# The order of a layer norm and MLP stage written out by hand, with part of its elementwise work moved to GpSimd

## The chip, the cores and the metric

The kernel runs on one core of a Trainium2 chip. The metric is the device time of one execution in microseconds (us); the time of a version is the median of several runs. The core has a matrix engine (TensorE, PE in the profile, with its weight loads as PEld), VectorE (DVE), ScalarE (ACT), GpSimd (POOL) and a queue engine that starts transfers (SyncE, SP). Each engine works through its own queue of instructions in order, and they wait for each other by semaphores. Matmul results land in PSUM, in banks of 512 f32 values for each of 128 partitions; everything else is in SBUF.

## The reference, cut to what matters

Four samples of 56 x 56 pixels with 128 channels go through four layers: a block of attention and MLP over windows, an edge layer, a spectral attention layer and a convolution, each behind a normalization. The change concerns only the second half of the first layer, which comes after its attention. For every pixel, with `h` the 128 values after attention and `x` the block's input:

```
n   = (h - mean(h)) / sqrt(var(h) + 1e-5) * g2 + be2       # over the 128 channels of a pixel
mlp = gelu(n @ w1 + b1) @ w2 + b2                          # 128 -> 512 -> 128
y   = h + mlp + x                                          # two residuals
```

The next layer normalizes `y` by groups of channels over the whole sample, so it needs the mean and variance of `y`.

## The kernel before, in words

All data is f32. `first_layers` runs once for each of the four samples, one after the other: `fast_attention`, then `mlp` (L848), then `edge_layer` (L905). Channels lie on the 128 partitions; a sample is a row of 3136 pixels in window order. `xf` holds `h`, `xw` holds `x`, and `x1` receives `y` in image order, from where the edge layer reads it. (A second branch of the program, for inputs with large scores, calls the same `mlp` and isn't executed.)

`mlp` cuts the sample into eight parts of 392 pixels, each a row of eight 7 x 7 windows. It has two stages:

- *The norm stage* (loop at L870). A matmul with a centring matrix subtracts the mean (`centre`, L676, matmul L679, into one of four PSUM banks `mm`). ScalarE squares the result into `n_sq` (L681) and copies it into `y` (L874). A second matmul averages the squares over the partitions (L689, into one of two banks `v`), ScalarE takes the square root (L691), VectorE the reciprocal (L692), and VectorE multiplies `y` by it (L877). The gains `g2` and `be2` are folded into the weights.
- *The MLP stage* (loop at L879). `hidden` (L860) makes four matmuls of a part (L864, into the banks `mm`) and four Gelu activations on ScalarE (L865). It is called for the part after the current one before the four matmuls of the current part with `w2` (L885), which add up in one of two banks `acc`, named `m_po`. VectorE then makes `h + b2 + x` in SBUF (L886) and adds it to the PSUM result while it puts the windows in image order: a large add for seven of the eight windows (343 pixels, L892) and two small ones for the eighth, which wraps around the side of the image (28 and 21 pixels, L894 and L895). A statistics instruction on the finished rows follows (L896). The last part goes in two pieces of four and three rows, since it wraps around the image.

A matmul of this size is two passes in the profile, so four matmuls are shown as "x8". TensorE's order is the program's order (`manual_schedule`, L868); the orders of ScalarE and VectorE in `mlp` are made by a list scheduler when the program is built. GpSimd has no work in `mlp`. ScalarE loads a table of functions when it turns from one to another: for the square root at L691, for Gelu at L865, and again for the square root by a dummy activation at L898. After `mlp`, `group_norm_factors` (L2348 to L2360) reduces the statistics, and the edge layer begins (L939).

Of the kernel before, what the change touches and what calls it, by code (L numbers as in the profile page):

```python
# [11 lines left out]
F32 = mybir.dt.float32  # L12
AF = mybir.ActivationFunctionType
ALU = mybir.AluOpType
# [4 lines left out]
P = 128  # L19
B = 4  # L20
HH = 56
# [651 lines left out]
        output(NBLK - 1, pm[:, :NB])  # L673


def centre(k, pool, centred, src, squares, j):  # L676

    nc = k.nc
    nc.tensor.matmul(centred, k.centre, src, start=True, stop=True)  # L679
    squares[j] = pool.tile([P, centred.shape[1]], F32, tag="sq", name="n_sq")  # L680
    nc.scalar.activation(squares[j], centred, AF.Square)  # L681


def inverse_deviation(k, pool, psum, squares, bufs=2):

    nc = k.nc
    n = squares.shape[1]
    pv = psum.tile([P, 512], F32, tag="v", name="n_pv")
    nc.tensor.matmul(pv[:, :n], k.ones_c, squares, start=True, stop=True)  # L689
    r = pool.tile([P, n], F32, tag="rs", name="n_r", bufs=bufs)  # L690
    nc.scalar.activation(r, pv[:, :n], AF.Sqrt, bias=k.eps)  # L691
    nc.vector.reciprocal(r, r)  # L692
    return r


def attention_bias(k, w, pool):


    nc = k.nc
    with k.tc.tile_pool(name="b_ps", bufs=1, space=PSUM) as psum:  # L700
        ps = psum.tile([P, 512], F32, name="b_p")
        nc.tensor.matmul(ps[:, 0:1], w.wo, w.bv, start=True, stop=True)
        for i, t in enumerate((w.wq, w.wk, w.wv)):
            nc.tensor.matmul(ps[:, 1 + i:2 + i], t, w.be1, start=True, stop=True)
        for f in range(4):
            nc.tensor.matmul(ps[:, 4 + f:5 + f], w.w1[:, f * P:(f + 1) * P], w.be2, start=True, stop=True)
        for n, t, g in (("fq", w.wq, w.g1), ("fk", w.wk, w.g1), ("fv", w.wv, w.g1), ("f1", w.w1, w.g2)):
            f = pool.tile(list(t.shape), F32, name="w_" + n)
            nc.vector.tensor_scalar_mul(f, t, g)
            setattr(w, n, f)  # L710
        for i, (n, bias) in enumerate((("bvo", w.bo), ("fbq", w.bq), ("fbk", w.bk), ("fbv", w.bv))):
            f = pool.tile([P, 1], F32, name="w_" + n)
            nc.vector.tensor_add(f, ps[:, i:i + 1], bias)
            setattr(w, n, f)
        w.fb1 = pool.tile([P, 4], F32, name="w_fb1")
        nc.vector.tensor_add(w.fb1, ps[:, 4:8], w.b1)
        nc.tensor.matmul(ps[:, 8:9], w.wo, w.fbv, start=True, stop=True)
        w.fbvo = pool.tile([P, 1], F32, name="w_fbvo")
        nc.vector.tensor_add(w.fbvo, ps[:, 8:9], w.bo)
# [128 lines left out]
def mlp(k, w, xf, xw, x1, st):  # L848


    nc, tc = k.nc, k.tc
    N = 8 * WIN
    with ExitStack() as es:
        big = es.enter_context(tc.tile_pool(name="m_big", bufs=1))
        wk = es.enter_context(tc.tile_pool(name="m_wk", bufs=2))
        psum = es.enter_context(tc.tile_pool(name="m_ps", bufs=2, space=PSUM))
        y = big.tile([P, TOK], F32, name="m_y")
        parts = [slice(wi * N, (wi + 1) * N) for wi in range(8)]

        def hidden(ts):  # L860
            hT = wk.tile([P, 4, N], F32, name="m_hT")
            for f in range(4):
                ph = psum.tile([P, 512], F32, tag="mm", name="m_ph", bufs=4)
                nc.tensor.matmul(ph[:, :N], w.f1[:, f * P:(f + 1) * P], y[:, ts], start=True, stop=True)  # L864
                nc.scalar.activation(hT[:, f, :], ph[:, :N], AF.Gelu, bias=w.fb1[:, f:f + 1])  # L865
            return hT

        es.enter_context(tc.manual_schedule(engines={mybir.EngineType.PE}))  # L868
        squares = {}
        for wi in range(9):  # L870
            if wi < 8:
                pc = psum.tile([P, 512], F32, tag="mm", name="m_pc", bufs=4)
                centre(k, wk, pc[:, :N], xf[:, parts[wi]], squares, wi)
                nc.scalar.copy(y[:, parts[wi]], pc[:, :N])  # L874
            if wi:
                yb = y[:, parts[wi - 1]]
                nc.vector.tensor_mul(yb, yb, inverse_deviation(k, wk, psum, squares.pop(wi - 1), 8))  # L877
        ahead = hidden(parts[0])
        for wi, ts in enumerate(parts):  # L879
            hT = ahead  # L880
            if wi < 7:
                ahead = hidden(parts[wi + 1])
            po = psum.tile([P, 512], F32, tag="acc", name="m_po")
            for f in range(4):
                nc.tensor.matmul(po[:, :N], w.w2[:, f, :], hT[:, f, :], start=(f == 0), stop=(f == 3))  # L885
            nc.vector.scalar_tensor_tensor(xf[:, ts], xf[:, ts], w.b2, xw[:, ts], ALU.add, ALU.add)  # L886
            a = xf[:, ts].rearrange("p (w i j) -> p w i j", w=8, i=7)
            x = po[:, :N].rearrange("p (w i j) -> p w i j", w=8, i=7)
            for i0, i1 in (((0, 7),) if wi < 7 else ((0, 4), (4, 7))):
                r0 = (7 * wi + 3 + i0) % HH  # L890
                rows = x1[:, r0:r0 + i1 - i0, :]
                nc.vector.tensor_add(  # L892
                    rows[:, :, 3:52].rearrange("p i (w j) -> p w i j", w=7), a[:, 0:7, i0:i1, :], x[:, 0:7, i0:i1, :])
                nc.vector.tensor_add(rows[:, :, 52:56], a[:, 7, i0:i1, 0:4], x[:, 7, i0:i1, 0:4])  # L894
                nc.vector.tensor_add(rows[:, :, 0:3], a[:, 7, i0:i1, 4:7], x[:, 7, i0:i1, 4:7])  # L895
                nc.vector.bn_stats(st[:, wi + (i0 > 0), :], rows.rearrange("p l n -> p (l n)"))  # L896

        nc.scalar.activation(wk.tile([P, 1], F32, name="m_root"), hT[:, 3, 0:1], AF.Sqrt, bias=k.eps, scale=0.0)  # L898

# [822 lines left out]
class Plan:  # L1724
# [8 lines left out]
    def add(self, engine, cost, run, after=(), takes=(), gives=(), lag=0.0, table=None):  # L1733
        op = Env()
        op.engine, op.cost, op.run, op.after, op.lag, op.table = engine, cost, run, list(after), lag, table
        op.takes, op.gives, op.end = list(takes), list(gives), None
        self.ops.append(op)
        return op
# [629 lines left out]
def build(k, packs, I, out):  # L2368
# [3 lines left out]
    with ExitStack() as es:  # L2372
# [12 lines left out]
        with tc.tile_pool(name="w01", bufs=1) as wp, tc.tile_pool(name="io", bufs=1) as io:  # L2385
# [30 lines left out]
            def first_layers(attention, x, to, loaded=False):  # L2416
                if not loaded:
                    nc.sync.dma_start(xw, x)
                xf = io.tile([P, TOK], F32, name="xf")
                attention(k, w0, xw, xf)  # L2420
                st = io.tile([P, 9, 6], F32, name="x1_st")
                mlp(k, w0, xf, xw, x1, st)
                edge_layer(k, w1, x1, st)
                nc.sync.dma_start(to, x1)
# [62 lines left out]
```

## Time and profile before

| what | value |
|---|---|
| median of 7 runs | 3905.01 us (3888.44 to 3908.33) |
| the profiled execution: own time, span of its instructions | 3898.99 us, 3897.2 us |
| busy: PE, DVE, ACT, POOL | 91%, 74%, 54%, 30% of the span |
| mean granted TensorE clock | 0.957 of full |

The span runs from the first instruction to the last; the execution's own time has 1.79 us more around it. Times of instructions are in us from the span's start. Where `mlp` lies in the four samples (us, from the timeline):

| sample | first centring matmul (L679) | first matmul of `hidden` of the second part (L864) | end of the last `w2` matmul (L885) | statistics reduced (L2348) |
|---|---|---|---|---|
| 1 | 535.81 | 551.79 | 595.52 | 597.20 |
| 2 | 1238.24 | 1254.58 | 1298.30 | 1299.98 |
| 3 | 1941.56 | 1957.81 | 2001.53 | 2003.22 |
| 4 | 2649.02 | 2664.98 | 2706.85 | 2708.54 |

So `mlp` takes some 61 us of each sample, about 245 us of the 3897. In a line of the timeline the first number is the start, the second the length, then come engine, line of the kernel, operation, destination and sources with their sizes and the number of instructions merged; in brackets stands the idle time before it and what ended that.

### The profile page before, as it was taken

Reading aid. Unit: us, or ns where it says so; the run is one execution under the profiler, and the core shown is the slowest. Engines: PE = TensorE matmul, PEld = TensorE weight load, DVE = VectorE, ACT = ScalarE, POOL = GpSimd, SP = SyncE. Lnnn points to the kernel's source line nnn. Section 1 sums busy time; section 2 is a strip of 40 time slices with the busy share of each in tenths; the row PEclk is TensorE's granted clock in tenths of the full one; section 3 lists DMA queues with packets and bytes.
Section 4 is the critical chain, followed back from the end, with each engine's and each line's share of the span. In section 5 each row is a group of like instructions: output and inputs, shape, how many; then the busy total and the mean of one; then the engine's idle time right before and its main releaser. Section 6 shows DMA issues by size and latency. Waiting matters only on the chain. (4 is left out here: it accounts for less than half of the span.)

```text
span 3897.2 us, 79417 instructions
## 1 busy us (share of the span) xinstructions
PE 3542.5 (91%) x35416; PEld 1593.6 (41%) x35416; DVE 2890.3 (74%) x2759; ACT 2086.6 (54%) x2108; POOL 1157.0 (30%) x563
## 2 busy tenths in 40 slices
PE   6899989989998898999889999998967989999988
PEld 4322234543223445222245532224446433336554
DVE  6588877758897784888778578886965767775664
ACT  4577755557786445877655467774622012215332
POOL 0000006500000470000037100001851768984665
PEclk8999999999999999999999999999978999999988
DMA  2000000000000000000000000000031048841101
GB/s 95 1 1 1 1 17 2 19 1 1 1 1 1 18 19 1 1 1 1 1 18 3 18 1 1 1 1 1 3 107 67 1 100 170 171 109 65 59 9 50
DMA packets 73497, 111.13 MB, mean 29 GB/s; under 512 B 62140, under 2 KB 63932, under 8 KB 67900
## 3 DMA queue, kind: packets, MB, share of 16 engines
q1 hardware_dynamic: 14460, 93.13, 8.1%
q10 hardware_dynamic: 58688, 12.85, 2.0%
q8 instruction: 280, 4.59, 0.5%
q14 instruction: 69, 0.57, 0.0%
HBM read 79.46 MB, written 26.51 MB: 27 GB/s over the span
## 5 line engine op out<-in xcount | busy, mean ns | idle before, releaser
L651 ACT ACTIVATE f_ring<-f_s 128x1792 f32<-128x1792 f32 (+3 forms) x796 | 1097.8, 1430 | 230.4 <-PE f_s L649 228.5
L594 DVE TENSOR_TENSOR f_acc<-f_acc,f_ring 128x1792 f32<-128x1792 f32 x560 | 1134.0, 2025 | 65.9 <-ACT f_ring L651 9.1
L988 POOL TENSOR_TENSOR e_tp<-e_a,e_c 128x1792 f32<-128x1792 f32 x140 | 451.6, 3258 | 2285.7 <-ACT e_a L951 2179.7
L649 PE MATMUL f_s<-f_qT,f_kT 32*128 32x448 f32 x5376 | 739.9, 572 | 48.1 <-ACT f_ring L651 28.3
L600 PE MATMUL f_po<-f_ring,f_va 128*32 128x448 f32 x5376 | 592.0, 548 | 0.0
L986 DVE TENSOR_TENSOR e_td<-e_pa,e_c 128x1792 f32<-128x1792 f32 x252 | 491.3, 2013 | 14.2 <-ACT e_a L951 14.2
L649 PEld LDWEIGHTS f_s<-f_qT,f_kT 32*128 32x128 f32 x5376 | 268.5, 183 | 526.7 <-ACT f_ring L651 383.1
L993 PE MATMUL e_acc<-e_td,t_shared 32*32 32x448 f32 x8064 | 323.0, 546 | 22.7 <-DVE e_td L986 11.7
L990 ACT ACTIVATE e_tp<-e_tp 128x1792 f32<-128x1792 f32 x140 | 235.1, 1697 | 176.5 <-POOL e_tp L988 176.5
L1589 DVE TENSOR_TENSOR u_ud<-u_px,u_d 112x1792 f32<-112x1792 f32 x144 | 240.1, 1707 | 95.3 <-PE u_po L1594 86.3
L600 PEld LDWEIGHTS f_po<-f_ring,f_va 128*32 128x32 f32 x5376 | 133.0, 109 | 398.5 <-issue 397.6
L993 PE MATMUL e_acc<-e_tp,t_shared 32*32 32x448 f32 x4480 | 221.9, 547 | 3.1 <-ACT e_tp L990 2.5
L1594 PE MATMUL u_po<-u_ud,AT 112*64 112x448 f32 x960 | 200.7, 548 | 23.3 <-DVE u_ud L1589 23.3
L1591 POOL TENSOR_TENSOR u_up<-xh,u_d 112x1792 f32<-112x1792 f32 x64 | 193.8, 3052 | 24.5 <-PE u_po L1594 12.9
L993 PEld LDWEIGHTS e_acc<-e_td,t_shared 32*32 32x32 f32 x8064 | 133.6, 103 | 147.1 <-DVE e_td L986 57.0
L617 DVE RECIPROCAL f_den<-f_den 128x448 f32<-128x448 f32 x28 | 82.7, 2953 | 77.5 <-ACT f_den L616 77.5
L1594 PE MATMUL u_po<-u_up,AT 112*64 112x448 f32 x576 | 125.0, 541 | 1.0 <-POOL u_up L1591 1.0
L1594 PEld LDWEIGHTS u_po<-u_ud,AT 112*64 112x64 f32 x960 | 64.8, 137 | 147.6 <-issue 86.6
L594 DVE TENSOR_TENSOR f_acc<-f_ring 128x1792 f32<-128x1792 f32 x28 | 56.7, 2024 | 89.2 <-ACT f_ring L651 60.3
L865 ACT ACTIVATE m_hT<-m_ph,w_fb 128x392 f32<-128x392 f32 x128 | 72.7, 589 | 84.3 <-PE m_ph L864 78.9
L993 PEld LDWEIGHTS e_acc<-e_tp,t_shared 32*32 32x32 f32 x4480 | 94.9, 103 | 55.5 <-ACT e_tp L990 19.5
L1678 ACT COPY x_ev<-x_po 56x896 f32<-56x896 f32 x32 | 28.8, 901 | 155.6 <-DMA xm<-x_ev 83.9
(467 smaller groups left out, 4763.3 us busy)
## 6 DMA issues: line engine op xcount, KB each, us to landing
u_d<-dd SPq DMA_DIRECT2D x48, 784.0 KB
xw<-in_x SPq DMA_DIRECT2D x4, 1568.0 KB
x2d<-x SPq DMA_DIRECT2D x4, 1568.0 KB
x_xs<-xad ACTq DMA_DIRECT2D x32, 196.0 KB
xm<-x_ev ACTq DMA_DIRECT2D x64, 98.0 KB
o_a<-xm SPq DMA_DIRECT2D x8, 784.0 KB
o_x<-x2d SPq DMA_DIRECT2D x4, 1568.0 KB
out<-o_o SPq DMA_DIRECT2D x12, 448.0 KB
```

What stands on the lines that cost most here:

```text
L594: nc.vector.tensor_add(acc, slots(j, 0) if c == 1 else acc, slots(j, c))
L600: nc.tensor.matmul(po[heads[h], :NB], va[o, c, heads[h]], p, start=(c == 0), stop=(c == 24))
L617: nc.vector.reciprocal(den[:, 0], den[:, 0])
L649: nc.tensor.matmul(ss[:, i, :NB], kT[heads[h], c * P:(c + 1) * P], qT[heads[h], blk(j)], start=True, stop=True)
L651: nc.scalar.activation(ring[:, slot:slot + m, :], ss[:, :m, :NB], AF.Exp, scale=scale)
L986: nc.vector.tensor_tensor(t, am, cm, ALU.max)
L988: nc.gpsimd.tensor_sub(t, bc(a.rearrange("p (l n) -> p l n", l=8), 1, 4), cm)
L990: nc.scalar.activation(tf, tf, AF.Relu)
L993: nc.tensor.matmul(acc[quarters[q], r, :NB], k.ident[o, o], t[o, q].rearrange("p l n -> p (l n)"), start=(g == 0), stop=(g == len(EDGE_TUR ...
L1589: nc.vector.tensor_mul(u, bc(px[:, :, :NB], 2, m), dm)
L1591: nc.gpsimd.tensor_mul(u, bc(x, 2, m), dm)
L1594: nc.tensor.matmul(po[64 * b2:64 * b2 + 64, :NB], st.AT[:, 8 * i + h0 + q, 2 * bp + b2, :], u[:, b2, q, :], start=(left == 16), stop=(left ...
```

## The change

Only `mlp` is changed; `centre` and `inverse_deviation`, which nothing else calls, are written into it.

- ScalarE and VectorE now follow the program's order in `mlp` too, like TensorE.
- The table of the square root is loaded by a dummy activation at the beginning of `mlp`. In ScalarE's queue of the built program it stands ahead of the last copy of the attention (`f_den`, L616); it waits for the last matmul of L608.
- Of the first four parts ScalarE squares the centred values, and VectorE copies them into `y`. Of the last four ScalarE copies them, and GpSimd squares the copy. The second matmul of a part follows its centring matmul at a distance of one for the first four parts and of two for the others.
- The reciprocals and multiplications of the parts 0 to 2 stand behind the four copies on VectorE; that of part `wi + 3` stands behind the `w2` matmuls of part `wi`.
- For the parts 0 to 6 VectorE adds PSUM, `b2` and `h` into SBUF in one instruction, and GpSimd adds `x` and puts the result in image order with three adds. Statistics of a part follow one turn later. Only the last part is written as before, its six adds ahead of its two statistics instructions.
- The load of the next sample's `xw` (L2418) now waits for GpSimd's last adds and for the last part's `h + b2 + x`.

```diff
@@ -673,26 +673,6 @@
         output(NBLK - 1, pm[:, :NB])
 
 
-def centre(k, pool, centred, src, squares, j):
-
-    nc = k.nc
-    nc.tensor.matmul(centred, k.centre, src, start=True, stop=True)
-    squares[j] = pool.tile([P, centred.shape[1]], F32, tag="sq", name="n_sq")
-    nc.scalar.activation(squares[j], centred, AF.Square)
-
-
-def inverse_deviation(k, pool, psum, squares, bufs=2):
-
-    nc = k.nc
-    n = squares.shape[1]
-    pv = psum.tile([P, 512], F32, tag="v", name="n_pv")
-    nc.tensor.matmul(pv[:, :n], k.ones_c, squares, start=True, stop=True)
-    r = pool.tile([P, n], F32, tag="rs", name="n_r", bufs=bufs)
-    nc.scalar.activation(r, pv[:, :n], AF.Sqrt, bias=k.eps)
-    nc.vector.reciprocal(r, r)
-    return r
-
-
 def attention_bias(k, w, pool):
 
 
@@ -865,37 +845,88 @@
                 nc.scalar.activation(hT[:, f, :], ph[:, :N], AF.Gelu, bias=w.fb1[:, f:f + 1])
             return hT
 
-        es.enter_context(tc.manual_schedule(engines={mybir.EngineType.PE}))
-        squares = {}
-        for wi in range(9):
+        es.enter_context(tc.manual_schedule(engines={mybir.EngineType.PE, mybir.EngineType.Activation,
+                                                     mybir.EngineType.DVE}))
+        squares, roots = {}, {}
+        root = wk.tile([P, 1], F32, name="m_root")
+        nc.scalar.activation(root, k.eps, AF.Sqrt)
+
+        def central(wi):
+
+            pc = psum.tile([P, 512], F32, tag="mm", name="m_pc", bufs=4)
+            yb = y[:, parts[wi]]
+            nc.tensor.matmul(pc[:, :N], k.centre, xf[:, parts[wi]], start=True, stop=True)
+            squares[wi] = wk.tile([P, N], F32, name="m_sq", bufs=3)
+            if wi < 4:
+                nc.scalar.activation(squares[wi], pc[:, :N], AF.Square)
+                nc.vector.tensor_copy(yb, pc[:, :N])
+            else:
+                nc.scalar.copy(yb, pc[:, :N])
+                nc.gpsimd.tensor_mul(squares[wi], yb, yb)
+
+        def deviation(wi):
+            pv = psum.tile([P, 512], F32, tag="v", name="m_pv")
+            nc.tensor.matmul(pv[:, :N], k.ones_c, squares.pop(wi), start=True, stop=True)
+            roots[wi] = wk.tile([P, N], F32, name="m_r", bufs=8)
+            nc.scalar.activation(roots[wi], pv[:, :N], AF.Sqrt, bias=k.eps)
+
+        def divide(wi):
             if wi < 8:
-                pc = psum.tile([P, 512], F32, tag="mm", name="m_pc", bufs=4)
-                centre(k, wk, pc[:, :N], xf[:, parts[wi]], squares, wi)
-                nc.scalar.copy(y[:, parts[wi]], pc[:, :N])
-            if wi:
-                yb = y[:, parts[wi - 1]]
-                nc.vector.tensor_mul(yb, yb, inverse_deviation(k, wk, psum, squares.pop(wi - 1), 8))
+                r = roots.pop(wi)
+                nc.vector.reciprocal(r, r)
+                nc.vector.tensor_mul(y[:, parts[wi]], y[:, parts[wi]], r)
+
+        for n in range(10):
+            if n < 8:
+                central(n)
+            if 1 <= n < 5:
+                deviation(n - 1)
+            elif n > 5:
+                deviation(n - 2)
+            if n == 3:
+                divide(0)
+        divide(1)
+        divide(2)
+
+        def image_rows(wi, i0, i1):
+            r0 = (7 * wi + 3 + i0) % HH
+            return x1[:, r0:r0 + i1 - i0, :]
+
+        def statistics(wi):
+            for i0, i1 in (((0, 7),) if wi < 7 else ((0, 4), (4, 7))):
+                nc.vector.bn_stats(st[:, wi + (i0 > 0), :], image_rows(wi, i0, i1).rearrange("p l n -> p (l n)"))
+
+        def windows(t):
+            return t.rearrange("p (w i j) -> p w i j", w=8, i=7)
+
         ahead = hidden(parts[0])
         for wi, ts in enumerate(parts):
             hT = ahead
             if wi < 7:
                 ahead = hidden(parts[wi + 1])
+            else:
+
+                nc.scalar.activation(root, k.eps, AF.Sqrt)
             po = psum.tile([P, 512], F32, tag="acc", name="m_po")
             for f in range(4):
                 nc.tensor.matmul(po[:, :N], w.w2[:, f, :], hT[:, f, :], start=(f == 0), stop=(f == 3))
-            nc.vector.scalar_tensor_tensor(xf[:, ts], xf[:, ts], w.b2, xw[:, ts], ALU.add, ALU.add)
-            a = xf[:, ts].rearrange("p (w i j) -> p w i j", w=8, i=7)
-            x = po[:, :N].rearrange("p (w i j) -> p w i j", w=8, i=7)
+            divide(wi + 3)
+            if wi < 7:
+                nc.vector.scalar_tensor_tensor(xf[:, ts], po[:, :N], w.b2, xf[:, ts], ALU.add, ALU.add)
+                if wi:
+                    statistics(wi - 1)
+                add, a, x = nc.gpsimd.tensor_add, windows(xf[:, ts]), windows(xw[:, ts])
+            else:
+
+                nc.vector.scalar_tensor_tensor(xf[:, ts], xf[:, ts], w.b2, xw[:, ts], ALU.add, ALU.add)
+                statistics(6)
+                add, a, x = nc.vector.tensor_add, windows(xf[:, ts]), windows(po[:, :N])
             for i0, i1 in (((0, 7),) if wi < 7 else ((0, 4), (4, 7))):
-                r0 = (7 * wi + 3 + i0) % HH
-                rows = x1[:, r0:r0 + i1 - i0, :]
-                nc.vector.tensor_add(
-                    rows[:, :, 3:52].rearrange("p i (w j) -> p w i j", w=7), a[:, 0:7, i0:i1, :], x[:, 0:7, i0:i1, :])
-                nc.vector.tensor_add(rows[:, :, 52:56], a[:, 7, i0:i1, 0:4], x[:, 7, i0:i1, 0:4])
-                nc.vector.tensor_add(rows[:, :, 0:3], a[:, 7, i0:i1, 4:7], x[:, 7, i0:i1, 4:7])
-                nc.vector.bn_stats(st[:, wi + (i0 > 0), :], rows.rearrange("p l n -> p (l n)"))
-
-        nc.scalar.activation(wk.tile([P, 1], F32, name="m_root"), hT[:, 3, 0:1], AF.Sqrt, bias=k.eps, scale=0.0)
+                rows = image_rows(wi, i0, i1)
+                add(rows[:, :, 3:52].rearrange("p i (w j) -> p w i j", w=7), a[:, 0:7, i0:i1, :], x[:, 0:7, i0:i1, :])
+                add(rows[:, :, 52:56], a[:, 7, i0:i1, 0:4], x[:, 7, i0:i1, 0:4])
+                add(rows[:, :, 0:3], a[:, 7, i0:i1, 4:7], x[:, 7, i0:i1, 4:7])
+        statistics(7)
 
 
 
```

## The prediction

> **What bounds the stage now.** The page comes first. TensorE is busy for most of the span, and a busy TensorE only gets faster where it waits or runs at a lower clock; so the next view is the waits, for TensorE alone. One line of it names the stage: four waits, one a sample, of a `w2` matmul on VectorE's last add.
>
> ```profile
> PE 3542.5 (91%) x35416; PEld 1593.6 (41%) x35416; DVE 2890.3 (74%) x2759; ACT 2086.6 (54%) x2108; POOL 1157.0 (30%) x563
> ```
> ```profile
> PE m_po L885 <- DVE x L895: 7.9, 4, 2.0
> ```
>
> The timeline of sample 1 shows where that wait lies.
>
> ```profile
> 562.43 2.80 PE L864 MATMUL m_ph<-m_y,w_f 128*128 128x392 f32 x8
> 565.53 0.97 DVE L877 TENSOR_TENSOR m_y<-m_y,n_r 128x392 f32<-128x392 f32 x2
> 566.42 0.50 DVE L892 TENSOR_TENSOR x<-xf,m_po 128x343 f32<-128x343 f32 x1
> ...
> 566.93 0.17 DVE L895 TENSOR_TENSOR x<-xf,m_po 128x21 f32<-128x21 f32 x1
> ...
> 567.25 4.57 PE L885 MATMUL m_po<-m_hT,t_first 128*128 128x392 f32 x8 [2.02 <-DVE x L895]
> ...
> 571.65 2.80 PE L864 MATMUL m_ph<-m_y,w_f 128*128 128x392 f32 x8
> ...
> 576.92 2.80 PE L864 MATMUL m_ph<-m_y,w_f 128*128 128x392 f32 x8
> ...
> 582.18 2.80 PE L864 MATMUL m_ph<-m_y,w_f 128*128 128x392 f32 x8
> ```
>
> TensorE has two banks for `m_po`. The third part needs the first one back, and that bank is emptied only at 566.93: VectorE works through all eight reciprocals (2.57 us each) and multiplications (0.53) before its first add from PSUM. After the wait the four matmuls take 4.57 us instead of 2.80. The windows of the same stretch say why (columns: stretch, length, busy PE, PEld, DVE, ACT, POOL, granted clock, DMA share, GB/s):
>
> ```profile
> 561.00:566.00 5.00, 4.23 (x13) 2.09 (x11) 5.00 (x4) 2.35 (x4) 0.00 (x0) 1.00 0.00 0
> 566.00:571.00 5.00, 3.75 (x7) 2.17 (x8) 4.25 (x13) 0.00 (x0) 0.00 (x0) 0.69 0.00 2
> 576.00:581.00 5.00, 5.00 (x17) 2.91 (x16) 1.26 (x4) 2.35 (x4) 0.00 (x0) 1.00 0.55 231
> ```
>
> VectorE is busy all through the first, and the granted clock falls from 1.00 to 0.69 behind the wait. In sample 4 the same wait passes without that:
>
> ```profile
> 2680.28 2.87 PE L885 MATMUL m_po<-m_hT,t_first 128*128 128x392 f32 x8 [1.86 <-DVE x L895]
> 2682.66 2.49 PEld L864 LDWEIGHTS m_ph<-m_y,w_f 128*128 128x128 f32 x8
> ```
>
> Outside this wait TensorE is the limit of the MLP stage: from 576.92 to 582.18 to 587.45 eight matmuls take 5.27 us again and again, 0.658 each, with ScalarE (2.56 of 5.27) and VectorE idle in between.
>
> **What is to be had.** From the first matmul of `hidden` of part 1 (551.79 in sample 1; held there by the first Gelu, not by VectorE) to the end of the stage, TensorE has 28 + 32 = 60 matmuls: 60 x 0.658 + 0.17 (from the last one's issue to its end, 2.80 - 2.63) = 39.7 us. The trace has 43.7, 43.7, 43.7 and 41.9 us in the four samples (table above). The excess is 4.0 + 4.0 + 4.0 + 2.2 = 14.2 us. Sample 4 shows how it splits: about 2.2 each is waiting (8.8 in all) and 1.8 in three samples is the lower clock (5.4).
>
> **Part by part.** *VectorE's new order.* Per part it has a reciprocal 2.57, a multiplication 0.53, the add from PSUM (0.60: the attention's add from PSUM, L623, takes 0.683 for 448 columns, and 0.683 x 392/448 = 0.60) and the statistics 0.57: 4.27, below TensorE's 5.27. Before the first division stand four copies from PSUM (0.57 by the copy of 128x392 at L424), each behind ScalarE's square. The fourth centring matmul ends at about 542.3, its square at 542.9, the copy at 543.5, so the divisions of parts 0, 1, 2, 3 end at about 546.6, 549.7, 552.8 and 555.9. Needed are they when `hidden` gets there: part 0 at 549.1, part 1 at 551.8, part 2 at 557.1. The `w2` matmuls of part 0 end at 557.1, VectorE empties the bank by 557.8, and TensorE wants it back at 565.0: the wait is gone with 7 us to spare, and nothing on VectorE comes late later, since each turn leaves it 1 us. Its statistics now wait for GpSimd, with the next reciprocal queued behind, but one turn (5.27) after adds that take some 1.3 us. So all 14.2 us go, unless another wait of about 2 us comes up.
>
> *The norm stage.* TensorE does the same 16 matmuls, back to back at 0.66 from 540.9 on, and the last of them started at 548.4 before, held by ScalarE's square. ScalarE loses eight squares and copies of 0.5 and the table load (1.28), which now runs behind the last L608 matmul, from 526.2 to 527.8 with the dummy activation, ahead of `f_den`, which can't start before 528.0: cost nothing, 0.2 us of cover, and without that cover at most 1.6 a sample. None of this shortens the stage, since TensorE is its limit. What is new is TensorE's wait for GpSimd's squares, with the rest of the norm and all of `hidden` queued behind: centring matmul of part 7 until 546.8, copy until 547.4, GpSimd, variance matmul. GpSimd's one row of 128x392 with two inputs (L2103) takes 0.84 us; by 128x448 (1.13) it would be 0.99. Alone, that puts the last variance matmul to 548.5. But GpSimd and VectorE get in each other's way:
>
> ```profile
> 3650.84 4.98 POOL L2254 TENSOR_TENSOR o_o<-o_s 128x896 f32<-128x896 f32 x3
> ...
> 3651.41 0.24 DVE L2020 RECIPROCAL o_r<-o_r 128x14 f32<-128x14 f32 x1 [0.65 <-ACT o_r L2016]
> 3651.57 4.28 DVE L2022 TENSOR_SCALAR o_e<-o_s,factors 128x7 f32<-128x7 f32 x1
> ```
> ```profile
> 2883.72 1.19 POOL L1385 TENSOR_TENSOR t_w_qk<-t_w_qk,q_skip 128x480 f32<-128x480 f32 x1
> 2883.86 1.12 DVE L1248 SCALAR_TENSOR_TENSOR s_sq<-s_d,s_sq 128x56 f32<-128x56 f32 x1
> ```
>
> L2022 takes 0.148 us by its median and 4.28 here, until GpSimd's three adds are over; L1248, with two SBUF inputs like the multiplication of a division, takes 1.12 instead of 0.21. The reciprocal L2020 (0.24 beside a median of 0.23) is not held. So the first multiplication, due at 546.05, meets GpSimd's squares and holds the last of them up by some 0.2: the last variance matmul starts at 548.7 instead of 548.4. I take **+0.3 us a sample**; bounds 0.1 (no meeting) and 0.75 (0.99 a square, and a whole multiplication in between). The root, the Gelu table and `hidden` of part 1 shift by the same.
>
> *The end.* Between the last two parts' `w2` matmuls lie 2.63 us. In them VectorE adds part 6 (0.60), GpSimd makes its three adds (0.84 x 343/392 = 0.74, then 0.25 and 0.24 by the 128x32 rows of L1374 and L1388; with 0.1 to start, 1.96 us after the part's matmuls), and VectorE still has `h + b2 + x` of part 7 (0.62, two SBUF inputs: held until 1.96) and the statistics of part 6 (0.57). The final adds can so start 3.0 us after part 6's matmuls instead of 2.66: **+0.35 us a sample**, bounds 0.0 and 1.4 (if the 343 in 49 pieces cost GpSimd twice as much). The six adds and two statistics after that are the same instructions (1.65 us in the table above).
>
> *Moved for nothing.* The next `xw` is requested after GpSimd's last add, at about 590 instead of 573; it moves in the windows from 571 to 581 and is read only by the next sample's attention, after an edge layer that ends its store at 753.8. SyncE's next entry is that store, far behind. GpSimd's queue is empty until the edge layer's first subtraction at 604.9.
>
> **The sum.** 14.2 - 4 x (0.3 + 0.35) = 11.6 us. The profiled execution took 3898.99 us, which gives 3887.4; it lies 6.0 us below the median of 3905.01, so 3893.4 for the median, 0.30% faster. About 0.2% (7.8 us) is what a measurement of this kernel can tell from no change. With both bounds the gain is 14.2 - 0.4 = 13.8 to 14.2 - 8.6 = 5.6, so 3891.2 to 3899.4.
>
> [...] The row is the 0.69 after a wait of 2.02 us; three of four such waits were followed by it. [...] The trace has the fall right behind the wait in three samples; the only other low clock in `mlp` is at its start, behind 5.8 us of idling. So I go by the row.
>
> **Rivals.** *The clock comes back elsewhere.* The fall depends on something not seen (sample 4 escaped with 1.86 us), and the change shifts everything after sample 1; slow stretches at the begin of `mlp` and of the edge layer could grow by what is saved. Then 8.8 - 2.6 = 6.2 is left: 3898.8. For it: sample 4. Against it: nothing else in the stage has a gap of 2 us.
>
> *Slower: GpSimd's squares stand behind the reciprocals.* If a reciprocal of 392 columns held GpSimd as L2022 was held, squares and divisions would alternate from 543.5 on: square 4 only after the first reciprocal (546.05), then 0.84, 0.53, 0.84, 2.57, 0.84, 0.53, 0.84. That sums to 6.99, so square 7 ends at 553.0 and the last variance matmul starts 4.65 us late; a TensorE idle for 4 us gets the lower clock for some 1.8 more. Per sample 4.65 + 1.8 + 0.35 - 3.55 = +3.25, in all 13 us: 3918. It decides from the point where that matmul comes 3.2 us late. Against it: L2020 beside L2254. For it: L2020 has 14 columns and proves little. [...] No row of the trace has a long reciprocal beside GpSimd.
>
> *The wait only moves*, to a division that comes late for `hidden` of part 1. The slack there is 551.8 - 549.7 = 2.1 us, the smallest of all; with the squares in between 1 us. Being late by that and 1 more would cost 4 us in all: 3897.
>
> **Chances.** The forecast 0.64, the moved wait 0.06, the clock elsewhere 0.18, slower by the reciprocals or something like it 0.12. The first two and a little of the clock's case are below 3897.2: faster 0.70. Same 0.18, slower 0.12. The range takes in the forecast's bounds and the clock's case, with some 5 us for the scatter of a median whose runs span 20 us: 3886 to 3904; outside are the slower case and a small part on the low side.
>
> **What would show it.** Right: TensorE's wait on VectorE at `m_po` is gone; the stretch from `hidden` of part 1 to the last `w2` matmul takes 39.7 us in all four samples, at clock 1.00; the last variance matmul starts 12.9 us after the first centring matmul (before: 12.6) and the last part's first add under 0.5 us after its matmuls. Wrong: GpSimd's squares at 2 us and more with ends that fall on those of reciprocals; a first `hidden` that waits for VectorE; a wait of VectorE's statistics on GpSimd at every part; or the same excess over 39.7 us in other places.

## The result, and the profile after

The changed kernel takes 3892.91 us (median of 18 runs, 3883.38 to 3900.26) against 3903.61 us for the kernel before in all of its runs (47 runs, 3888.44 to 3917.05). Compared on the same chips, the ratio is 0.9969, with a 95% interval of 0.9961 to 0.9978: 12.1 us faster (8.6 to 15.2); the medians are 10.7 apart. Predicted were 3893.4 us and 11.6 us.

The profiled execution of the changed kernel took 3903.09 us (span 3901.3), not the 3887.4 that the sum gave for it, and more than the 3898.99 of before. So the two profiles can't be compared by their spans; they are compared by stage. From the first line of the page the busy time of an engine is to be read: GpSimd has 53 us of new work, TensorE is busy for 10 us longer although its instructions are the same, which is clock and not work.

```profile
PE 3552.7 (91%) x35416; PEld 1598.2 (41%) x35416; DVE 2888.5 (74%) x2691; ACT 2079.3 (53%) x2080; POOL 1210.0 (31%) x663
```

The waits of TensorE in `mlp` (waiting engine, tile and line, releaser, us in all, times, longest us). Of its tiles only this line is left, one wait a sample at the very start, which the kernel before has too; the line of `m_po` on VectorE is gone.

```profile
PE m_pc L858 <- DVE xf L623: 3.5, 4, 0.9
```

The timeline where the wait was, sample 1. VectorE empties the bank of part 0 from 564.45 to 565.08, with divisions still to come, and TensorE, which needs it at 572.15, runs on without a bracket:

```profile
561.62 2.80 PE L912 MATMUL m_po<-m_hT,t_first 128*128 128x392 f32 x8
564.25 2.80 PE L844 MATMUL m_ph<-m_y,w_f 128*128 128x392 f32 x8
564.45 0.63 DVE L915 SCALAR_TENSOR_TENSOR xf<-m_po,t_first,xf 128x392 f32<-128x392 f32 x1 [1.34 <-PE m_po L912]
564.99 2.59 DVE L876 RECIPROCAL m_r<-m_r 128x392 f32<-128x392 f32 x1
...
572.15 2.80 PE L912 MATMUL m_po<-m_hT,t_first 128*128 128x392 f32 x8
574.78 0.49 PE L844 MATMUL m_ph<-m_y,w_f 128*128 128x392 f32 x1
```

The windows from the first matmul of `hidden` of part 1 to the end of the last `w2` matmul, one row a sample (columns: stretch, length, busy PE, PEld, DVE, ACT, POOL, granted clock, DMA share, GB/s): TensorE is busy for all 39.77 us at clock 1.00. Before, the same four stretches took 43.73, 43.72, 43.72 and 41.87.

```profile
558.88:598.65 39.77, 39.77 (x121) 22.71 (x120) 24.83 (x27) 19.03 (x33) 9.59 (x21) 1.00 0.00 0
1258.79:1298.56 39.77, 39.77 (x121) 22.71 (x120) 24.83 (x27) 19.03 (x33) 9.59 (x21) 1.00 0.00 0
1959.58:1999.35 39.77, 39.77 (x121) 22.71 (x120) 24.83 (x27) 19.03 (x33) 9.57 (x21) 1.00 0.00 0
2662.13:2701.90 39.77, 39.76 (x121) 22.71 (x120) 24.82 (x27) 19.03 (x33) 9.58 (x21) 1.00 0.00 1
```

By these times `mlp` divides into three stretches (us, samples 1 to 4; sums are of unrounded times):

| stretch | before | after | difference |
|---|---|---|---|
| first centring matmul to `hidden` of part 1 | 15.98, 16.34, 16.25, 15.96 | 16.80, 16.62, 15.57, 16.17 | +0.63 |
| from there to the end of the last `w2` matmul | 43.72, 43.72, 43.72, 41.87 | 39.77 four times | -13.96 |
| from there to the statistics reduced | 1.69 four times | 1.78, 1.78, 1.77, 1.79 | +0.38 |
| sum | 244.31 | 231.36 | -12.95 |

The rest of the execution was 17 us longer in this profile, in work that the change doesn't touch: up to the first centring matmul 542.08 us instead of 535.81, behind the last `mlp` 1197.6 instead of 1188.6. The experiments below ask whether that belongs to the change.

### The profile page after: what moved, and what is told of

Its sections match the earlier page's. It is cut to its first block, busy times and chain, and to the rows that moved or that the text cites. A ratio compares the mean times of both kernels' runs of the same rounds, so it can differ in the third digit from the quotient of the medians.

```text
span 3901.3 us, 79427 instructions
## 1 busy us (share of the span) xinstructions
PE 3552.7 (91%) x35416; PEld 1598.2 (41%) x35416; DVE 2888.5 (74%) x2691; ACT 2079.3 (53%) x2080; POOL 1210.0 (31%) x663
## 5 line engine op out<-in xcount | busy, mean ns | idle before, releaser
L865 POOL TENSOR_TENSOR m_sq<-m_y 128x392 f32<-128x392 f32 x16 | 14.5, 920 | 1949.3 <-ACT m_y L864 1949.2
L1024 PE MATMUL e_acc<-e_td,t_shared 32*32 32x448 f32 x8064 | 322.4, 545 | 21.3 <-DVE e_td L1017 10.4
```

The costliest lines, as they stand in the source:

```text
L1024: nc.tensor.matmul(acc[quarters[q], r, :NB], k.ident[o, o], t[o, q].rearrange("p l n -> p (l n)"), start=(g == 0), stop=(g == len(EDGE_TUR ...
```

## The experiments

Two theories stood at the start. Mine: the gain is TensorE's wait for a free `m_po` bank with the clock fall behind it, so anything that takes this wait away gives all of it, and GpSimd's part gives nothing. The rival: the elementwise work moved to GpSimd is worth something by itself, or takes away from the gain. A single execution scatters by some 10 us, so the verdicts on the mechanism rest on the stretches of `mlp`, and three versions were also timed in rounds.

**A third bank and nothing else.** The kernel before, with one bank less for `mm` and one more for `m_po`.

```diff
-                ph = psum.tile([P, 512], F32, tag="mm", name="m_ph", bufs=4)
+                ph = psum.tile([P, 512], F32, tag="mm", name="m_ph", bufs=3)
-                pc = psum.tile([P, 512], F32, tag="mm", name="m_pc", bufs=4)
+                pc = psum.tile([P, 512], F32, tag="mm", name="m_pc", bufs=3)
-            po = psum.tile([P, 512], F32, tag="acc", name="m_po")
+            po = psum.tile([P, 512], F32, tag="acc", name="m_po", bufs=3)
```

> The kernel before, with its scheduled order and no GpSimd work in mlp, but three PSUM banks for m_po and three instead of four for the centred values and the hidden parts. The theory (the gain is TensorE's wait for a free m_po bank, and the lower clock behind it): the wait is gone, the stretch from hidden of part 1 to the last w2 matmul takes 39.7 us in all samples, as in the changed kernel and 43.7 before, at clock 1.00; the stretch before it grows by one matmul (0.66) in each sample, since only three hidden matmuls fit ahead of the first Gelu. mlp over the four samples: 244.3 - 14.2 + 2.6 = 232.7 us. Rival (the gain comes from less work on VectorE, so the old order still stalls): over 42 us for that stretch.

The timeline of this kernel in sample 1: VectorE's first add from PSUM is as late as before (566.45; it was 566.42), but the third part's matmuls start at 565.93 with nothing ahead of them and take 2.80, not 4.57.

```profile
563.30 2.80 PE L864 MATMUL m_ph<-m_y,w_f 128*128 128x392 f32 x8
...
565.93 2.80 PE L885 MATMUL m_po<-m_hT,t_first 128*128 128x392 f32 x8
566.45 0.50 DVE L892 TENSOR_TENSOR x<-xf,m_po 128x343 f32<-128x343 f32 x1
...
571.20 2.80 PE L885 MATMUL m_po<-m_hT,t_first 128*128 128x392 f32 x8
```

The middle stretch took 39.66 us in every sample at clock 1.00, and `mlp` 232.29 in all. The missing `mm` bank shows as a new wait of TensorE for a Gelu, 0.6 us once a sample, ahead of the middle stretch:

```profile
PE m_ph L864 <- ACT m_hT L865: 2.4, 4, 0.6
```

Three numbers changed give 12.0 of the 12.95 us. Timed in five rounds:

> The kernel before with three banks for m_po and three for the hidden parts, timed. The theory (its mlp took 232.3 us against 244.3 before and 231.4 in the changed kernel): a median 9 to 13 us below the kernel before, within 3 us of the changed kernel. Rival (a gain in the stage is lost behind it): less than 6 us.

3891.22 us (6 runs) beside 3907.68 for the kernel before, ratio 0.9962 (0.9948 to 0.9976, or 9.4 to 20.3 us), `mlp` 232.97. The medians are 16.5 us apart, more than the 9 to 13 expected, which the interval includes. In time it can't be told from the change.

**The squares back on ScalarE**, all else as in the change.

```diff
             else:
+                nc.scalar.activation(squares[wi], pc[:, :N], AF.Square)
                 nc.scalar.copy(yb, pc[:, :N])
-                nc.gpsimd.tensor_mul(squares[wi], yb, yb)
```

> The changed kernel with the squares of parts 4 to 7 on ScalarE again, each ahead of ScalarE's copy, nothing else changed. The theory (GpSimd's squares give nothing, since TensorE and ScalarE set the norm stage): the last variance matmul starts within 0.3 us of the changed kernel's (12.1 to 13.3 us after the first centring matmul, 12.8 in the mean), the stretch behind it stays at 39.8. Rival (ScalarE's load was the limit of the norm stage, and GpSimd relieves it): the last variance matmul starts 1 us or more later in each sample, 4 us in all.

`mlp` took 231.14 us in all against 231.36: GpSimd's squares bring nothing (one run, 3897.86).

**Every GpSimd square twice**, to see what they cost if they were slower.

```diff
                 nc.gpsimd.tensor_mul(squares[wi], yb, yb)
+                nc.gpsimd.tensor_mul(squares[wi], yb, yb)
```

> The changed kernel with each of GpSimd's four squares made twice, to see what its squares cost once they are on the path. The theory (0.84 us each, back to back from the first copy on, not held by the reciprocals): the last square ends at 8 x 0.84 = 6.7 us after GpSimd's first start instead of 4.1, so the last variance matmul starts 2.6 us later than in the changed kernel, 10.4 us in all, and the stretch behind it stays at 39.8. mlp over the four samples 241.8 us, still under the 244.3 of the kernel before. Rival (squares and reciprocals exclude each other): 4.5 us and more later in each sample, and mlp above 248 us.

Now GpSimd is what the norm stage waits for; its queue in sample 1, with L866 the second copy:

```profile
549.95 0.84 POOL L865 TENSOR_TENSOR m_sq<-m_y 128x392 f32<-128x392 f32 x1
550.87 1.04 POOL L866 TENSOR_TENSOR m_sq<-m_y 128x392 f32<-128x392 f32 x1
551.87 0.83 POOL L865 TENSOR_TENSOR m_sq<-m_y 128x392 f32<-128x392 f32 x1
552.79 0.84 POOL L866 TENSOR_TENSOR m_sq<-m_y 128x392 f32<-128x392 f32 x1
```

and the wait that it makes:

```profile
PE m_pv L870 <- POOL m_sq L866: 10.4, 16, 1.0
```

The first stretch is 2.7 to 3.3 us longer in each sample, `mlp` 243.64: almost the whole gain is gone, 12.3 us where 10.4 were expected. By its timeline GpSimd's eight squares run from 548.23 to 555.54 almost without a pause, 7.3 us instead of the 6.7 expected (two of them take 1.04), and TensorE waits for each second one.

**All parts written from PSUM by VectorE**, in the hand order (GpSimd keeps the squares).

```diff
-            if wi < 7:
-                nc.vector.scalar_tensor_tensor(xf[:, ts], po[:, :N], w.b2, xf[:, ts], ALU.add, ALU.add)
...
-                add, a, x = nc.gpsimd.tensor_add, windows(xf[:, ts]), windows(xw[:, ts])
-            else:
...
+            nc.vector.scalar_tensor_tensor(xf[:, ts], xf[:, ts], w.b2, xw[:, ts], ALU.add, ALU.add)
+            add, a, x = nc.vector.tensor_add, windows(xf[:, ts]), windows(po[:, :N])
...
+            if wi < 7:
+                statistics(wi)
         statistics(7)
```

> The changed kernel with all parts written from PSUM by VectorE, as before the change, but in the order written by hand: divisions three parts ahead, then h + b2 + x, the three adds and the statistics of the part; squares of the last four parts stay on GpSimd. The theory (the order alone frees the bank in time): VectorE has 4.9 us of work in each turn of 5.27, TensorE never waits, 39.8 us for the stretch from hidden of part 1 in all samples, and the end of mlp as before (1.69 us from the last w2 matmul to the reduced statistics; 1.78 in the changed kernel). Rival (without GpSimd's adds VectorE is too slow): waits at m_po come back, over 40.5 us.

39.77 us in every sample, the last stretch 1.56 instead of 1.78, `mlp` 230.79 (one run, 3901.1). VectorE has time for all of it.

**Neither**: both edits together, so that `mlp` has the order by hand and no GpSimd. Timed in five rounds.

> The order written by hand alone, without any GpSimd work in mlp: squares of all parts on ScalarE, all parts written from PSUM by VectorE. The theory (the order carries the whole gain): mlp over the four samples 230.6 us (231.4 in the changed kernel, 244.3 before), 39.8 us from hidden of part 1 to the last w2 matmul in every sample; the median 10 to 13 us below that of the kernel before. Rival (GpSimd's part carries some of it): mlp above 233 us and a median less than 8 us below.

3891.66 us (6 runs) beside the same 3907.68, ratio 0.9957 (0.9941 to 0.9974, or 10.2 to 23.1 us; 16.0 by the medians, where 10 to 13 were expected); middle stretch 39.77 four times, `mlp` 231.34. The order by hand alone gives what the change gives, as far as these runs can tell.

**The last part's `h + b2 + x` one turn earlier**, which takes away the wait that the prediction charged with 0.35 us a sample.

```diff
             if wi < 7:
+                if wi == 6:
+                    nc.vector.scalar_tensor_tensor(xf[:, parts[7]], xf[:, parts[7]], w.b2, xw[:, parts[7]], ALU.add, ALU.add)
                 nc.vector.scalar_tensor_tensor(xf[:, ts], po[:, :N], w.b2, xf[:, ts], ALU.add, ALU.add)
...
-                nc.vector.scalar_tensor_tensor(xf[:, ts], xf[:, ts], w.b2, xw[:, ts], ALU.add, ALU.add)
                 statistics(6)
```

> The changed kernel with VectorE's h + b2 + x of the last part moved one turn ahead, before the add of part 6 from PSUM, into time in which VectorE idles. The theory (at the end of mlp this sum and GpSimd's adds hold each other up, 1.02 us for it instead of 0.62 and 0.58 instead of 0.25 for GpSimd's second add): the sum takes 0.62 us, GpSimd's adds of part 6 take 0.91, 0.25 and 0.24 us, the first final add starts 0.04 us after the last w2 matmul instead of 0.28, and the time from that matmul to the reduced statistics falls from 1.78 to about 1.55 us, 0.9 us in all. Rival (the GpSimd adds alone are the limit there): the first final add still starts 0.2 us late or more.

The first final add starts 0.04 us after the matmuls instead of 0.28, the last stretch takes 1.56, `mlp` 229.93, the shortest of all. Timed:

> The changed kernel with the last part's sum moved one turn ahead, timed; its mlp took 229.9 us against 231.4. The theory: a median 11 to 15 us below the kernel before, not told apart from the changed kernel or from the two variants without GpSimd's work (all within 3 us of each other). Rival (GpSimd's or the sum's place matters beyond mlp): more than 4 us from them.

3889.95 us (9 runs) beside 3906.34, ratio 0.9969 (0.9956 to 0.9981): 12.1 us (7.4 to 17.2), or 16.4 by the medians, just outside the 11 to 15 expected. Its `mlp` took 230.74 in this profile. The 0.9 us that it should gain over the change are below what these runs can tell, and its interval overlaps with those of the third bank and of the version without GpSimd: of the four versions none is shown to be the fastest.

**The kernel before, profiled again**, for the 17 us in stages that nobody touched.

> The kernel before, profiled once more, for the scatter of what the change doesn't touch. The theory (the lower clock behind the wait is a matter of where the wait falls, and the same kernel differs from run to run by such stretches elsewhere): 43.7 us from hidden of part 1 to the last w2 matmul in some samples and 41.9 in the others, nothing between; the time behind mlp of sample 4 differs from the 1188.6 us of the first profile by several us (1195 to 1204 in the four profiles of kernels that are the same there). Rival (the change and the variants lengthen the later layers): 1188.6 us again, within 1.

The middle stretch was 43.72, 43.72, 43.72 and 41.86 again, in `mlp` 244.86; behind the last `mlp` it took 1195.4 us, not 1188.6, and the execution 3907.3. All that lies outside `mlp` took 3660.6 us here and 3652.9 in the first profile: the unchanged kernel alone differs by 7.8, the changed one (3669.9) by 17.1. The records of the granted clock account for both. Outside `mlp` TensorE was at half clock for 305.4 us in the first profile of before, for 318.0 in this one and for 339.5 in that of the changed kernel. If half of that time is loss, 3500.2, 3501.7 and 3500.2 us are left. So the 17 us are stretches at half clock and not other work. They differ by execution: the kernel with the last sum moved, which is the change but for the place of one instruction, had 309.9 and 308.2 us of them in its two profiles; the other versions lie between 309.5 and 342.3.

**A wait of chosen length.** Why did sample 4 escape the clock fall? Its wait is the shortest, 1.86 against 2.02. In the version without GpSimd a reciprocal that nothing reads was put ahead of the first add from PSUM, of a different length in each sample, and the divisions of parts 3 to 5 ahead of that.

```diff
+HOLD = (362, 440, 596, 673)
...
+            if wi == 0:
+                for ahead_ in (3, 4, 5):
+                    divide(ahead_)
...
+                hold = wk.tile([P, 768], F32, name="m_hold", bufs=1)
+                nc.vector.reciprocal(hold[:, :held], y[:, :held])
```

> How long may TensorE wait before its clock falls? The order by hand without GpSimd, where VectorE makes the divisions of parts 3 to 5 and then a useless reciprocal of a chosen width (362, 440, 596 and 673 columns in samples 1 to 4) before it adds part 0 from PSUM, so that TensorE waits some 1.0, 1.5, 2.5 and 3.0 us for the m_po bank. The theory (the clock falls behind a wait of about 2 us): the stretch from hidden of part 1 to the last w2 matmul is 39.8 plus the wait in samples 1 and 2, and 39.8 plus the wait plus 1.8 in samples 3 and 4, with clock 1.00 and under 0.97. [...]

The waits came out shorter than meant. The timeline of TensorE in the four samples (the bracket is the wait):

```profile
569.84 2.87 PE L918 MATMUL m_po<-m_hT,t_first 128*128 128x392 f32 x8 [0.30 <-DVE x L933]
...
1269.79 2.87 PE L918 MATMUL m_po<-m_hT,t_first 128*128 128x392 f32 x8 [0.79 <-DVE x L933]
...
1970.86 1.56 PE L918 MATMUL m_po<-m_hT,t_first 128*128 128x392 f32 x4 [1.77 <-DVE x L933]
...
2674.50 4.56 PE L918 MATMUL m_po<-m_hT,t_first 128*128 128x392 f32 x8 [2.26 <-DVE x L933]
```

The middle stretch grew by the wait and 0.24 us in the first three samples (40.31, 40.80, 41.78), and by 1.69 us more in the fourth (43.96). Sample 3, where a fall was expected, had none, at a wait of 1.77. So it was sized again, with 616, 622, 628 and 647 columns:

> The order by hand without GpSimd, with a reciprocal that nothing reads (616, 622, 628 and 647 columns in samples 1 to 4) ahead of the first h+b2+x, sized from the run with 362 to 673 columns so that TensorE's wait for the bank comes to about 1.90, 1.94, 1.98 and 2.10 us. Theory that the clock falls behind a wait of some 2 us: the stretch from the first hidden matmul of part 1 to the last second-layer matmul is 39.77 + 0.24 us + the wait where the clock stays (41.9 to 42.0), and about 1.9 us more where it falls (43.9 to 44.1); it falls in sample 4 at 2.10, and the samples ahead of it say where between 1.86 and 2.02 the change lies. [...] Second rival, that it is the place within the clock's own window and not the length: falls without order by length, for instance in sample 1 and not in sample 3.

```profile
567.17 4.57 PE L918 MATMUL m_po<-m_hT,t_first 128*128 128x392 f32 x8 [1.90 <-DVE x L933]
...
1272.87 4.43 PE L918 MATMUL m_po<-m_hT,t_first 128*128 128x392 f32 x8 [1.93 <-DVE x L933]
...
1976.37 4.57 PE L918 MATMUL m_po<-m_hT,t_first 128*128 128x392 f32 x8 [1.97 <-DVE x L933]
...
2683.40 4.57 PE L918 MATMUL m_po<-m_hT,t_first 128*128 128x392 f32 x8 [2.09 <-DVE x L933]
```

The clock fell in all four, at 1.90 us too: 43.60, 43.63, 43.67 and 43.79, each 1.69 us above 39.77, the wait and 0.24 (1.9 were expected). With the 1.86 and 1.85 us of sample 4 in the two profiles of before, which had no fall, the change lies between 1.86 and 1.90 for this wait. Over the 16 waits of these four profiles the falls are in order of length (none up to 1.86, all from 1.90 on), which speaks for the first theory. The second rival, the place of the wait, isn't tested by them, since all 16 lie whole within one window of the clock's grid. Another wait in the same traces does test it, and the place matters: see the last section.

## Why the prediction was right, point by point

The sum was 14.2 - 1.2 - 1.4 = 11.6 us; its terms measured 13.96 - 0.63 - 0.38 = 12.95 in `mlp`, and the timed runs show 12.1. That 3893.4 and 3892.91 agree to half a microsecond is luck: the interval of 8.6 to 15.2 us can't tell 11.6 from 12.95, the two costs were charged with 2.6 us and measured 1.0, and the prediction started from a median of 3905.01 of 7 runs, which 47 runs put at 3903.61.

**The excess in the middle stretch** was the reason, and of the right size: 13.96 us gone, 14.2 predicted. 39.77 us at clock 1.00 in all samples is the 39.7 of the sum. The third bank and the version without GpSimd show that the wait for the bank carries all of it: with either alone the stretch is 39.66 or 39.77.

**The split into waiting and clock.** The prediction put the clock down to the wait by its row (0.69 after a wait of 2.02 us). The measurement bears it out: in this place waits of 1.90 to 2.26 us halved the clock (1.00 to 0.50), every time. (The idling at the start of `mlp` that the prediction put at 5.8 us is 5.11 and 0.87 us in the trace, with one matmul between.)

**The norm stage** cost less than charged. The prediction named one number, 12.9 us from the first centring to the last variance matmul; measured were 13.30, 13.12, 12.07 and 12.67. This length hangs on how long the clock is still halved at the start of `mlp`, which differs by sample and execution. Taking half of the time at half clock off it (the passes of a matmul then start 0.65 us apart instead of 0.33, so half of it is loss) leaves 10.27, 10.27, 10.27 and 10.26 after, and 10.08, 10.07 and 10.08 in the first three samples before (10.24 in the fourth, where 12.46 seems a floor; 12.46 also recurs in the run with three banks). At equal clock the change costs about 0.2 us a sample instead of 0.3. The mechanism that was charged is there, as the timeline of the changed kernel shows: a multiplication beside GpSimd takes 0.76 instead of 0.57, and of GpSimd's 16 squares, 0.84 by the median, the longest takes 1.16. TensorE is held by the last two squares, too shortly for the list of waits: the weights of the last two variance matmuls are loaded only when a square has ended (555.37 after 552.50 + 2.81 = 555.31).

```profile
550.38 2.59 DVE L876 RECIPROCAL m_r<-m_r 128x392 f32<-128x392 f32 x1
551.24 0.84 POOL L865 TENSOR_TENSOR m_sq<-m_y 128x392 f32<-128x392 f32 x1 [488.55 <-ACT m_y L864]
...
552.50 2.81 POOL L865 TENSOR_TENSOR m_sq<-m_y 128x392 f32<-128x392 f32 x3 [0.42 <-ACT m_y L864]
553.01 0.76 DVE L877 TENSOR_TENSOR m_y<-m_y,m_r 128x392 f32<-128x392 f32 x1
553.72 2.58 PE L869 MATMUL m_pv<-m_sq,c_ones_c 128*128 128x392 f32 x6
554.52 0.30 PEld L869 LDWEIGHTS m_pv<-m_sq,c_ones_c 128*128 128x128 f32 x2 [0.61 <-POOL m_sq L865]
...
555.37 0.30 PEld L869 LDWEIGHTS m_pv<-m_sq,c_ones_c 128*128 128x128 f32 x2 [0.56 <-POOL m_sq L865]
```

With the squares back on ScalarE the same figure is 10.33, no better: there the last variance matmul waits for a root of ScalarE, since the two banks `v` are still taken.

```profile
550.33 0.93 PE L869 MATMUL m_pv<-m_sq,c_ones_c 128*128 128x392 f32 x2 [0.25 <-ACT m_r L871]
```

**The slower rival falls** on the first two lines of the timeline of the changed kernel above: the square from 551.24 to 552.08 lies inside a reciprocal that takes the usual 2.59. No row of the kernel before had shown a long reciprocal beside GpSimd; here the two ran beside each other at their medians, the square in 0.84 and the reciprocal in 2.59. The run with doubled squares shows what squares of twice the time cost: 12.3 us, nearly the gain.

**The end** is the term that was mis-sized: +0.35 us a sample predicted, +0.09 measured. The waits came as described, VectorE's sum beside GpSimd's adds (1.02 instead of 0.62) and its statistics behind them:

```profile
596.76 0.91 POOL L926 TENSOR_TENSOR x<-xf,xw 128x343 f32<-128x343 f32 x1 [3.94 <-DVE xf L915]
597.07 1.02 DVE L921 SCALAR_TENSOR_TENSOR xf<-xf,t_first,xw 128x392 f32<-128x392 f32 x1
597.63 0.58 POOL L927 TENSOR_TENSOR x<-xf,xw 128x28 f32<-128x28 f32 x1
...
598.44 0.57 DVE L897 BATCH_NORM_STATS2 x_st<-x 128x6 f32<-128x392 f32 x1 [0.34 <-POOL x L928]
598.92 0.34 DVE L926 TENSOR_TENSOR x<-xf,m_po 128x196 f32<-128x196 f32 x1
...
599.71 0.62 DVE L897 BATCH_NORM_STATS2 x_st<-x 128x6 f32<-128x224 f32 x2
600.43 0.40 DVE L2379 BATCH_NORM_AGGREGATE gf_mv<-x_st 128x2 f32<-128x54 f32 x1
```

The first final add starts 0.28 us after the last matmul (598.64, by its end), not 0.04 as before: +0.24, against 0.34 predicted. What the prediction left out is that the six adds and two statistics are not "the same instructions" in time: both statistics now stand behind all adds and run without a pause between them, 1.51 us from the first add to the reduction where 1.65 were charged. GpSimd's 343-pixel add takes 0.91 us, not the 0.74 scaled from a whole row; in windows of 7 x 7 it takes 2.65 ns a pixel, in the squares of whole rows 2.14.

**The clock comes back elsewhere**: not in `mlp`. The time at half clock at the start of `mlp`, over four samples, is 20.1 us before and 20.2 after, and behind that the clock is 1.00. For the rest of the kernel the timed runs speak: 12.1 of the 12.95 us arrive, and with the interval's 8.6 a loss of more than some 4 us elsewhere is excluded, a smaller one is not. **The wait only moves**: no wait of `hidden` on VectorE appears.

**The time of the profiled execution** (3887.4 predicted, 3903.09 measured) was wrong, while the median was met. A sum against one execution gives the difference; the level of the next execution is its own.

## What to carry to other kernels

When one wait of an engine that sets the pace ends on a shared buffer, price the number of buffers before the order of the work: here one bank more for the results, taken from the other matmuls, gave a time that can't be told from that of a rewritten stage with a fourth engine. Moving elementwise work to an idle engine was worth nothing here, where the engine that it left had slack; it added waits between the two (of VectorE for GpSimd's last add 1.4 us over the four samples). And where the untouched stages scatter by more than the edit is worth, compare stage by stage, and take the level from timed rounds.

## What the runs showed of the hardware

**The clock fell behind waits of 1.90 us.** In the records the granted clock is 1.0 or 0.5, in stretches that are multiples of 3.41 us, on a grid that runs on through the execution. The windows below are cut on that grid: TensorE's busy time in the 3.41 us that hold the wait, and the clock in the next. With a wait of 1.90 us (the first sample of the second sized run):

```profile
564.06:567.47 3.41, 1.51 (x5) 0.68 (x4) 3.38 (x5) 1.70 (x3) 0.00 (x0) 1.00 0.00 0
567.47:570.88 3.41, 3.41 (x6) 1.69 (x5) 2.48 (x7) 0.00 (x0) 0.00 (x0) 0.50 0.00 0
570.88:574.29 3.41, 3.41 (x12) 1.98 (x11) 2.48 (x5) 1.71 (x3) 0.00 (x0) 1.00 0.00 0
```

and with 1.86 us, sample 4 of the kernel before:

```profile
2677.35:2680.76 3.41, 1.54 (x6) 0.67 (x5) 3.41 (x8) 1.55 (x3) 0.00 (x0) 1.00 0.00 0
2680.76:2684.17 3.41, 3.41 (x12) 2.02 (x11) 3.41 (x11) 0.32 (x1) 0.00 (x0) 1.00 0.02 5
```

Busy for 1.51 of 3.41 us is followed by half clock, 1.54 is not. Idling for some 55% of such a window was enough here, in 11 of 11 waits for the `m_po` bank of 1.90 us and more. A fall costs 1.69 us, half of the 3.41 (1.71); the prediction's 1.8 was the difference of 43.7 and 41.9, in which 0.16 is a longer wait (2.02 against 1.86).

**The same wait with and without a fall.** All 16 waits of the four profiles compared above lay whole within one window of the grid. A wait at the start of the next sample's attention (L360) doesn't always: it takes 2.12 us in the kernel before and in the changed one, where the grid lies otherwise. First the kernel before, where it lies whole in the window from 752.24 on:

```profile
755.10 1.11 PE L360 MATMUL w_mm<-w_xg,t_first 128*128 128x392 f32 x2 [2.12 <-DVE w_xg L192]
```
```profile
752.24:755.65 3.41, 1.29 (x4) 0.46 (x4) 2.56 (x3) 0.00 (x0) 2.46 (x5) 1.00 0.36 155
755.65:759.07 3.42, 3.42 (x20) 1.96 (x18) 2.71 (x4) 0.58 (x1) 3.31 (x12) 0.50 0.75 315
```

Then the changed kernel, where the grid cuts it at 756.36 into 0.34 and 1.78 us:

```profile
758.14 0.90 PE L360 MATMUL w_mm<-w_xg,t_first 128*128 128x392 f32 x2 [2.12 <-DVE w_xg L192]
```
```profile
756.36:759.77 3.41, 1.63 (x6) 0.82 (x8) 3.41 (x4) 0.00 (x0) 3.41 (x8) 1.00 0.69 294
759.77:763.19 3.42, 0.95 (x16) 0.71 (x14) 2.68 (x4) 1.13 (x2) 3.31 (x8) 1.00 0.41 176
```

In the profiles of all versions this wait of 2.12 us occurs 32 times at full clock. In 14 it lies whole within one window, and the clock falls 14 times; in 18 the grid cuts it, and it falls in none. So neither the length alone nor the place alone goes with the fall, but the idling within one window. Sample 4 of `mlp`, which escaped by what the prediction called "something not seen", escaped by the length: its TensorE came 0.16 us later out of the norm stage (10.24 against 10.08 at equal clock), so its wait was 1.86 us. How much idling is needed differs by place: a cut wait with 1.97 us in one window (1.45 us busy, the changed kernel at 1456.10) left the clock at 1.00, and in the kernel before the window from 3595.55 on, busy for 2.69 us with other shapes, was followed by half clock. The 1.51 and 1.54 are no limit for other places, and what exactly the clock counts is open.

**The level of an execution goes with the clock.** Of the runs of the changed kernel the one of 3883.38 us had a mean granted clock of 0.960, the one of 3900.26 us 0.953; the profiled execution had 0.954, that of before 0.957. What puts more half-clock stretches into one execution than into another is open.
